# Edge stage of a convolution network: all five maps on VectorE, their sums on ScalarE, weights in batches of one to four images

## The chip, the core and the metric

The kernel runs on one core of one Trainium2 chip, in float32. The metric is the device time of one execution in microseconds. A core has TensorE (PE; its weight loads are shown apart as PEld), VectorE (DVE), ScalarE (ACT), GpSimd (POOL), and SyncE (SP), whose queue issues most DMAs. Each engine runs its own instructions in order and waits for others by semaphores.

## The reference, cut to what matters

The network has a graph layer, a deformable convolution with a state-space scan, a convolution, and last an edge-guided U-shaped network. Only the first layer of that last one, here called the edge stage, is touched. Its input x is 16 images of 32 channels, 128 x 128, after a group norm:

```python
def _norm(x):
    m = jnp.mean(x, axis=(1, 2, 3), keepdims=True)
    s = jnp.std(x, axis=(1, 2, 3), keepdims=True)
    return (x - m) / s

def get_operator(x):
    p3 = ((1, 1), (1, 1))
    p2 = ((1, 0), (1, 0))
    b1 = _norm(0.5 * _corr(x, SOBEL_X, p3) + 0.5 * _corr(x, SOBEL_Y, p3))
    b2 = _norm(0.5 * _corr(x, SCHARR_X, p3) + 0.5 * _corr(x, SCHARR_Y, p3))
    b3 = _norm(_corr(x, LAPLACE3, p3))
    b4 = _norm(0.5 * _corr(x, ROBERTS_X, p2) + 0.5 * _corr(x, ROBERTS_Y, p2))
    b5 = _norm(0.5 * _corr(x, PREWITT_X, p3) + 0.5 * _corr(x, PREWITT_Y, p3))
    return jnp.concatenate([b1, b2, b3, b4, b5], axis=1)
```

These 160 channels go through a 3 x 3 convolution to 32 channels and a 2 x 2 maximum. Every map is a fixed small stencil (with reflected borders), normalised by one mean and one deviation per image and map.

## The kernel before, in words

The network's layers run one after another: `layer0`, `layer1_offsets`, `layer1_scan`, `layer1_sample`, `layer2`, `layer3_edges` (the edge stage), `layer3_net`. Images stand in four groups of four.

The edge stage does not convolve the 160 maps. A stencil followed by a 3 x 3 convolution is one 5 x 5 convolution of x, and normalising a map only scales its part of the weights. So the stage needs, for each image, the mean and variance of the five maps; from these it builds that image's 5 x 5 weights, and convolves x itself with them. Three kinds of work follow:

- Statistics, the generator `stats`. An image is loaded in two strips (h = 0, 1), each a tile `a` with 4 bands of 32 channels on the 128 partitions and 18 rows of 130. From a strip come five maps of 16 x 128 per partition: f1 (Sobel), f2 (Scharr, held in E2), f3 (Laplace), f4 (Roberts), f5 (Prewitt), by way of the sums R, B2, H and differences E1, E2. GpSimd makes E1, E2 and H, VectorE the rest; `keep` runs four bn_stats on each finished map (line 1570), and bn_aggr closes an image. The generator yields after a few operations, so that the caller can place them between convolutions.
- Weights, the function `weights`, for a group of four images: the norm factors (`ms` line 1618, PE averages `pm`, `pv`, a square root on ScalarE), the small diagonal matrices l4 and l5, and twenty matmuls `pw` (lines 1647 and 1648) of the fixed tables base4 and base5, whose results ScalarE copies to Eb and Bb. Then `pr`, `rm`, `pvec`, `pb` give border terms. `expand` copies an image's rows of Eb and Bb by 14 DMAs on SP's queue into W and Wb.
- Convolution of an image: `image` loads it as tile t and scales it on ScalarE (line 1695), `corrections` makes border terms `pc`, `cs`, and `conv` runs eight times: ten matmuls into one of four PSUM buffers `ps` (line 1767), then VectorE adds `cs` at the border columns (line 1785) and takes maxima of pairs into `pl` (line 1786). ScalarE's queue stores `pl` to `p1`.

The driver at the end of `layer3_edges` makes the statistics and weights of group 0, and then, during the convolutions of images 0 to 2 of a group, takes one step of the next group's statistics after an even convolution and two after an odd one; before image 3's convolutions it takes the rest and makes the next group's weights. What the source writes is then placed by a scheduler that lays each engine's instructions in a fixed order of its own, so that operations stand near, but not exactly at, their place in the source. Tile buffers (pool sizes `bufs`) limit how far one engine runs ahead of another.

Of the kernel before, what the change touches and what calls it, by code (L numbers as in the profile page):

```python
# [10 lines left out]
F32 = mybir.dt.float32  # L11
# [6 lines left out]
P = 128  # L18
# [1417 lines left out]
def layer3_edges(tc, w, x3, p1, sb3, b3, groups=range(NG)):  # L1436
# [10 lines left out]
    with ExitStack() as ctx:  # L1447
# [112 lines left out]
        def stats(g, res):  # L1560

            mv = sp.tile([P, 4, 5, 2], F32, name="mv", tag="mv")
            res["mv"] = mv
            nxt = strip(g, 0, 0)
            for j in range(4):
                st = sp.tile([P, 5, 8, 6], F32, name="st", tag="st")

                def keep(i, h, f):
                    for q in range(4):
                        V.bn_stats(st[:, i, 4 * h + q], f[:, 4 * q : 4 * q + 4])  # L1570

                for h in range(2):
                    a = nxt
                    E2 = fp.tile([P, 16, HW], F32, name="E2", tag="e", bufs=2)
                    nc.gpsimd.tensor_sub(E2, a[:, 2:18, 2 : HW + 2], a[:, 0:16, 0:HW])
                    E1 = fp.tile([P, 16, HW], F32, name="E1", tag="e", bufs=2)
                    nc.gpsimd.tensor_sub(E1, a[:, 0:16, 2 : HW + 2], a[:, 2:18, 0:HW])
                    R = fp.tile([P, 18, HW + 1], F32, name="R", tag="R")
                    V.tensor_add(R, a[:, :, 0 : HW + 1], a[:, :, 1 : HW + 2])
                    B2 = fp.tile([P, 17, HW + 1], F32, name="B2", tag="B2")  # L1580
                    V.tensor_add(B2, R[:, 0:17], R[:, 1:18])
                    f1 = fp.tile([P, 16, HW], F32, name="f1", tag="f", bufs=2)
                    V.tensor_sub(f1, B2[:, 1:17, 1 : HW + 1], B2[:, 0:16, 0:HW])
                    yield
                    keep(0, h, f1)
                    f4 = fp.tile([P, 16, HW], F32, name="f4", tag="f", bufs=2)
                    V.tensor_sub(f4, R[:, 1:17, 0:HW], R[:, 0:16, 0:HW])
                    keep(3, h, f4)
                    yield
                    if h == 0:  # L1590
                        nxt = strip(g, j, 1)
                    elif j < 3:
                        nxt = strip(g, j + 1, 0)
                    V.scalar_tensor_tensor(E2, E2, -0.4, f1, ALU.mult, ALU.add)
                    keep(1, h, E2)
                    f5 = fp.tile([P, 16, HW], F32, name="f5", tag="f", bufs=2)
                    V.tensor_sub(f5, B2[:, 0:16, 1 : HW + 1], B2[:, 1:17, 0:HW])
                    V.tensor_add(f5, f5, E1)
                    yield
                    keep(4, h, f5)  # L1600
                    H = fp.tile([P, 18, HW], F32, name="H", tag="H")
                    nc.gpsimd.tensor_add(H, a[:, :, 2 : HW + 2], a[:, :, 0:HW])
                    f3 = fp.tile([P, 16, HW], F32, name="f3", tag="f", bufs=2)
                    V.tensor_add(f3, H[:, 2:18], H[:, 0:16])
                    V.scalar_tensor_tensor(
                        f3, a[:, 1:17, 1 : HW + 1], -4.0, f3, ALU.mult, ALU.add
                    )
                    keep(2, h, f3)
                    yield
                for i in range(5):  # L1610
                    V.bn_aggr(mv[:, j, i], st[:, i])

        def weights(g, mv):


            sc = cb[:, g, :, 0].unsqueeze(2).to_broadcast([P, 4, 5])
            ms = sp.tile([P, 4, 5], F32, name="ms", tag="ms")
            V.tensor_mul(ms, mv[:, :, :, 0], sc)
            vs = sp.tile([P, 4, 5], F32, name="vs", tag="vs")
            V.tensor_mul(vs, mv[:, :, :, 1], sc)  # L1620
            V.tensor_mul(vs, vs, sc)
            pm = psg.tile([P, 4, 5], F32, name="pm", tag="pg")
            nc.tensor.matmul(pm, avg, ms, start=True, stop=True)
            mean = sp.tile([P, 4, 5], F32, name="mean", tag="mean")
# [4 lines left out]
            pv = psg.tile([P, 4, 5], F32, name="pv", tag="pg")  # L1629
            nc.tensor.matmul(pv, avg, ms, start=True, stop=True)  # L1630
            r = sp.tile([P, 4, 5], F32, name="r", tag="r")
# [4 lines left out]
            rs = sp.tile([P, 4, 5], F32, name="rs", tag="rs")  # L1636
            V.tensor_mul(rs, r, isel.unsqueeze(1).to_broadcast([P, 4, 5]))
            r4 = sp.tile([P, 4], F32, name="r4", tag="r4")
            V.reduce_sum(r4, rs, AX.X)
            ey = eye.unsqueeze(1).to_broadcast([P, 4, T])  # L1640
            l4 = sp.tile([P, 4, T], F32, name="l4", tag="l4")
            V.tensor_mul(l4, ey, r4.unsqueeze(2).to_broadcast([P, 4, T]))
            l5 = sp.tile([P, 4, T], F32, name="l5", tag="l5")
            V.tensor_mul(l5, ey, r[:, :, 4].unsqueeze(2).to_broadcast([P, 4, T]))
            for n, ((a, m), (q, o)) in enumerate(zip(cuts, place)):
                pw = psg.tile([P, 480], F32, name="pw", tag="pg")
                nc.tensor.matmul(pw[:, 0:m], l4, base4[:, a : a + m], start=True, stop=False)
                nc.tensor.matmul(
                    pw[:, 0:m], l5[32 * q : 32 * q + 32], base5[32 * q : 32 * q + 32, o : o + m],
                    start=False, stop=True,  # L1650
                )
                if n < 4:
                    nd = m // 160
                    nc.scalar.copy(
                        Eb[:, 3 * n : 3 * n + nd, 3:8],
                        pw[:, 0:m].rearrange("p (d y o) -> p d y o", d=nd, o=T),
                    )
                else:
                    nc.scalar.copy(Bf[:, n - 4], pw[:, 0:m])

            pr = psg.tile([5, P], F32, name="pr", tag="pg")
            for j in range(4):
                nc.tensor.matmul(
                    pr, mean[0:1, j], oneh[:, j], start=(j == 0), stop=(j == 3)
                )
            rm = sp.tile([5, P], F32, name="rm", tag="rm")
            V.tensor_copy(rm, pr)
            pvec = psg.tile([P, 15, T], F32, name="pvec", tag="pg")
            nc.tensor.matmul(pvec, rm, V5, start=True, stop=True)
            vec = sp.tile([P, 15, T], F32, name="vec", tag="vec")  # L1670
            nc.scalar.copy(vec, pvec)
            pb = psg.tile([P, 1], F32, name="pb", tag="pg")
            for j in range(4):
                nc.tensor.matmul(
                    pb[32 * j : 32 * j + 32], V5[:, 14], rm[:, 32 * j : 32 * j + 1],
                    start=True, stop=True, tile_position=(0, 32 * j),
                )
            V.tensor_add(b3[:, g : g + 1], pb, bcol)
# [112 lines left out]
        res = {}  # L1791
        for _ in stats(groups[0], res):
            pass
        vec = weights(groups[0], res["mv"])
        nxt = image(groups[0], 0), *expand(0)
        for m, g in enumerate(groups):
# [3 lines left out]
            for j in range(4):  # L1800
# [3 lines left out]
                elif more:  # L1804
                    for _ in it:
                        pass
# [3 lines left out]
                for n in range(8):  # L1810
# [4 lines left out]
                    if n % 2:  # L1815
                        next(it, None)
# [459 lines left out]
```

## Time and profile before

| | |
|---|---|
| median of 3 runs | 17622.46 us (17619.95 to 17635.37) |
| profiled execution | 17609.38 us, of which the span 17607.6 us |
| PE busy in the span | 15472.8 us (88%) |
| DVE busy | 14994.4 us (85%) |
| ACT busy | 11513.4 us (65%) |
| POOL busy | 10390.4 us (59%) |
| first R of the edge stage (line 1579) | starts at 14888.6 us |
| bn_stats (line 1570) | 640 of them, 395.8 us busy |
| E2, E1, H on POOL (lines 1575, 1577, 1602) | 32 each, means 6662, 5515 and 5790 ns |

All times inside the profile are microseconds from the start of the span, means of one instruction are nanoseconds. A row of a group of instructions reads: line, engine, operation, output and input by name, shapes, count, then busy time and mean of one, then the idle time of the engine just before them and what ended it. A timeline row reads: start, length, engine, line, operation. A row of the stretches reads: stretch, length, then busy time and instruction count of PE, PEld, DVE, ACT and POOL, the granted clock of TensorE as a share of full speed, the busy share of the DMA engines, and GB/s. Matmuls overlap in the pipeline and a float32 matmul shows as two records, so PE's pace is read from starts, not from durations.

### The profile page before, as it was taken

The page shows a single profiled execution, that of the slowest core. Times are in us where ns is not written, and L with a number is a line of the kernel's source. Part 1 is how long each engine was busy: PE and PEld are TensorE (multiplying, and loading weights), DVE is VectorE, ACT ScalarE, POOL GpSimd, SP SyncE. Part 2 cuts the span into 40 slices and gives each one's busy share as a digit, 9 for nine tenths or more (in the row PEclk, how much of TensorE's full clock was granted, in tenths as well). Part 3 has the DMA queues.
Part 4 walks back from the last instruction along what each step waited for, and adds up shares of the span by engine and source line. Part 5 has one row for each costly group of instructions (what it writes and reads, how often), then busy time and mean ns, then how long its engine had stood idle before and what let it go on. Part 6 is the DMA issues. An engine that isn't in the chain of part 4 may idle for free. (4 is left out here: it accounts for less than half of the span.)

```text
span 17607.6 us, 299698 instructions
## 1 busy us (share of the span) xinstructions
PE 15472.8 (88%) x113450; PEld 5973.3 (34%) x113450; DVE 14994.4 (85%) x15134; ACT 11513.4 (65%) x22768; POOL 10390.4 (59%) x18561
## 2 busy tenths in 40 slices
PE   8999999999999888888888888899999976488988
PEld 3333333333333222222222222355555542144433
DVE  9999999999999769999999999788888877999123
ACT  7888888888888556776777777689888952000011
POOL 9999999999999437788888888200000001443000
PEclk9999999999999989999999999889999988699988
DMA  0000000000000664444454445677777788244245
GB/s 21 11 12 11 12 17 11 12 11 12 16 12 7 105 142 157 160 161 156 163 166 164 164 160 167 164 192 199 200 194 195 198 185 173 49 75 73 52 125 174
DMA packets 1519822, 1884.46 MB, mean 107 GB/s; under 512 B 146789, under 2 KB 866717, under 8 KB 1507558
## 3 DMA queue, kind: packets, MB, share of 16 engines
q1 hardware_dynamic: 1413414, 1688.04, 37.2%
q10 hardware_dynamic: 78336, 83.90, 1.5%
q0 software_dynamic: 26624, 93.35, 1.5%
q8 instruction: 892, 14.61, 0.3%
q14 instruction: 556, 4.55, 0.1%
HBM read 1561.58 MB, written 229.64 MB: 102 GB/s over the span
## 5 line engine op out<-in xcount | busy, mean ns | idle before, releaser
L235 POOL TENSOR_SCALAR Rp<-su,nv 128x128 f32<-128x128 f32 x16384 | 5837.5, 374 | 71.7 <-PE pS L241 37.8
L224 DVE TENSOR_TENSOR Rd<-pu,nv 128x2048 f32<-128x2048 f32 x2176 | 4882.9, 2279 | 75.4 <-PE pS L241 71.6
L239 ACT ACTIVATE Ra<-su,bv 128x128 f32<-128x128 f32 x14336 | 4295.0, 395 | 534.6 <-PE pS L241 530.4
L241 PE MATMUL pS<-Rd,zw 128*32 128x512 f32 x17408 | 2910.6, 603 | 214.7 <-DVE Rd L224 214.4
L822 DVE TENSOR_TENSOR_SCAN hh<-dd,state,pd 128x512 f32<-128x512 f32 x2304 | 2823.8, 1267 | 152.0 <-PE py L856 8.5
L843 POOL TENSOR_TENSOR hh<-hh,bc 128x2048 f32<-128x2048 f32 x512 | 2319.9, 4531 | 462.7 <-DVE state L830 452.7
L241 PE MATMUL pS<-Rp,zw 128*32 128x512 f32 x8192 | 2015.9, 597 | 175.6 <-POOL Rp L235 173.6
L1228 POOL DMA_DIRECT2D x<-ob x64 | 90.9, 1420 | 3094.0 <-DVE ob L1227 2757.2
L807 PE MATMUL pd<-du,spread 32*128 32x512 f32 x4608 | 1349.7, 660 | 563.1 <-DVE hh L822 556.0
L799 ACT ACTIVATE dd<-dd,m_a 128x512 f32<-128x512 f32 x2304 | 1518.1, 715 | 358.0 <-DMA dd<-dm 348.6
L817 DVE TENSOR_TENSOR pd<-pd,bc 128x1024 f32<-128x1024 f32 x1152 | 1401.7, 1217 | 55.1 <-ACT bc L780 54.4
L241 PE MATMUL pS<-Ra,zw 128*32 128x512 f32 x7168 | 1278.2, 600 | 0.0
L1236 ACT ACTIVATE yd<-yd,nrow 128x2048 f32<-128x2048 f32 x512 | 1234.5, 2411 | 47.4 <-DMA yd<-ymap 47.4
L1767 PE MATMUL ps<-t,W 128*128 128x512 f32 x2560 | 1170.4, 617 | 88.6 <-DVE pl L1786 88.6
L1116 ACT ACTIVATE ya<-pb,nrow 128x1024 f32<-128x1024 f32 x1024 | 1192.8, 1255 | 74.5 <-PE pb L1115 74.2
L1115 PE MATMUL pb<-Y,sel 32*128 32x512 f32 (+1 forms) x5120 | 1080.9, 741 | 167.5 <-ACT ya L1116 164.3
L241 PEld LDWEIGHTS pS<-Rd,zw 128*32 128x32 f32 x17408 | 624.3, 109 | 1222.1 <-issue 590.6
L807 PEld LDWEIGHTS pd<-du,spread 32*128 32x128 f32 x4608 | 373.4, 191 | 1607.5 <-DVE hh L822 719.0
L1120 DVE TENSOR_SCALAR yd<-yd 128x2048 f32<-128x2048 f32 x512 | 727.0, 1420 | 201.6 <-ACT yd L1236 200.4
L241 PEld LDWEIGHTS pS<-Rp,zw 128*32 128x32 f32 x8192 | 444.6, 110 | 1326.7 <-POOL Rp L235 865.1
L1120 DVE TENSOR_SCALAR ya<-ya 128x2048 f32<-128x2048 f32 x512 | 756.9, 1478 | 10.5 <-ACT ya L1116 9.4
L1767 PEld LDWEIGHTS ps<-t,W 128*128 128x128 f32 x2560 | 498.2, 197 | 724.1 <-issue 723.1
(403 smaller groups left out, 23453.0 us busy)
## 6 DMA issues: line engine op xcount, KB each, us to landing
dd<-dm SPq DMA_DIRECT2D x2304, 256.0 KB
yd<-ymap SPq DMA_DIRECT2D x512, 1024.0 KB
hw<-x SPq DMA_DIRECT2D x192, 512.0 KB
dm<-dt POOLq DMA_DIRECT2D x192, 256.0 KB, 3.6
xb<-tok SPq DMA_DIRECT2D x248, 144.0 KB
w<-d SPq DMA_DIRECT2D x64, 528.1 KB
x<-in_x SPq DMA_DIRECT2D x64, 512.0 KB
x<-o SPq DMA_DIRECT2D x128, 256.0 KB
```

The costliest lines, as they stand in the source:

```text
L224: nc.vector.tensor_tensor(R, st["pu"].unsqueeze(1).to_broadcast([P, 4, 4, HW]), nv[:, :, i::32].rearrange("p t q -> p q t").unsqueeze(3).t ...
L235: nc.gpsimd.tensor_scalar(R[:, q, k], su[:, k], 3.4028234e38, nv[:, k, c], ALU.min, ALU.max)
L239: nc.scalar.activation(R[:, q, k], su[:, k], AF.Relu, bias=bv[:, k, c])
L241: nc.tensor.matmul(st["pS"][32 * q : 32 * q + 32], zw[:, 31 - i : 63 - i], R[:, q], start=first, stop=False, tile_position=(0, 32 * q), sk ...
L799: S.activation(dd[:, r], dd[:, r], AF.Exp, scale=acol[:, dr, d : d + 1])
L807: nc.tensor.matmul(pd[:, a], spread[e, k], st["du"][n][e], start=True, stop=True)
L817: V.tensor_mul(pd, pd, bm.unsqueeze(1).to_broadcast([P, 2, CH]))
L822: V.tensor_tensor_scan(hh[:, r, s], dd[:, r, s], pd[:, a, s], st["state"][:, 4 * i + r : 4 * i + r + 1], ALU.mult, ALU.add,)
L843: G.tensor_mul(hh, hh, st["bc"][1, n].unsqueeze(1).to_broadcast([P, 4, CH]))
L1120: V.tensor_scalar(t, t, 1.0, 1.0, ALU.min, ALU.subtract)
L1236: S.activation(yd, yd, AF.Abs, bias=nrow)
L1767: nc.tensor.matmul(ps, W[:, k, d], t[:, 4 * n + k : 4 * n + k + 4, d : d + HW], start=(i == 0), stop=(i == 9 and n not in (0, 7)), skip_gr ...
```

## The change

In `stats`, the differences f2 and E1 and the sum H move from GpSimd to VectorE, bn_stats and bn_aggr go, and ScalarE makes for each map its sum (an Identity with an accumulated output), the negative mean of the strip's map, and the sum of squared deviations (a Square with that bias, accumulated). Six small VectorE operations per image combine the two strips into mean and variance. Maps have five buffers in place of two and two. The next strip is loaded a strip ahead.

`weights` takes a range of images instead of a group, with outputs at those images' partitions only. The driver runs over single images; the batches are image 0, 1, 2-3, 4-5, 6-7, 8-11 and 12-15. A batch is made after the fifth convolution of the image before it, after the statistics it needs; two steps of the statistics follow each convolution, up to a pace that is set for images from 6 on.

```diff
-                    nc.gpsimd.tensor_sub(E2, a[:, 2:18, 2 : HW + 2], a[:, 0:16, 0:HW])
-                    nc.gpsimd.tensor_sub(E1, a[:, 0:16, 2 : HW + 2], a[:, 2:18, 0:HW])
...
-                        V.bn_stats(st[:, i, 4 * h + q], f[:, 4 * q : 4 * q + 4])
...
-                    nc.gpsimd.tensor_add(H, a[:, :, 2 : HW + 2], a[:, :, 0:HW])
...
-                    V.bn_aggr(mv[:, j, i], st[:, i])
+                def keep(i, f):
+                    nm = sp.tile([P, 1], F32, name="nm", tag="nm", bufs=4)
+                    nc.scalar.activation(f, f, AF.Identity, accum_out=sq[:, 0, h, i : i + 1])
+                    nc.scalar.mul(nm, sq[:, 0, h, i : i + 1], -1.0 / (16 * HW))
+                    nc.scalar.activation(
+                        f, f, AF.Square, bias=nm, accum_out=sq[:, 1, h, i : i + 1]
+                    )
+                R = made("R", 18, HW + 1)
+                V.tensor_add(R, a[:, :, 0 : HW + 1], a[:, :, 1 : HW + 2])
+                f4 = made("f")
+                V.tensor_sub(f4, R[:, 1:17, 0:HW], R[:, 0:16, 0:HW])
+                keep(3, f4)
+                yield
+                B2 = made("B2", 17, HW + 1)
+                V.tensor_add(B2, R[:, 0:17], R[:, 1:18])
+                f1 = made("f")
+                V.tensor_sub(f1, B2[:, 1:17, 1 : HW + 1], B2[:, 0:16, 0:HW])
+                yield
+                f2 = made("f")
+                V.tensor_sub(f2, a[:, 2:18, 2 : HW + 2], a[:, 0:16, 0:HW])
+                V.scalar_tensor_tensor(f2, f2, -0.4, f1, ALU.mult, ALU.add)
+                keep(0, f1)
+                keep(1, f2)
+                yield
+                E1 = made("f")
+                V.tensor_sub(E1, a[:, 0:16, 2 : HW + 2], a[:, 2:18, 0:HW])
+                f5 = made("f")
+                V.tensor_sub(f5, B2[:, 0:16, 1 : HW + 1], B2[:, 1:17, 0:HW])
+                yield
+                V.tensor_add(f5, f5, E1)
+                keep(4, f5)
+                H = made("R", 18, HW + 1)[:, :, 0:HW]
+                V.tensor_add(H, a[:, :, 2 : HW + 2], a[:, :, 0:HW])
+                yield
+                f3 = made("f")
+                V.tensor_add(f3, H[:, 2:18], H[:, 0:16])
+                V.scalar_tensor_tensor(
+                    f3, a[:, 1:17, 1 : HW + 1], -4.0, f3, ALU.mult, ALU.add
+                )
+                keep(2, f3)
+                yield
...
-        def weights(g, mv):
+        def weights(b0, b1, mv):
+            g, j0 = divmod(b0, 4)
+            n = b1 - b0
+            e = slice(32 * j0, 32 * (j0 + n))
...
+                nc.tensor.matmul(
+                    pw[e, 0:m], l4, base4[:, a : a + m], start=True, stop=False,
+                    tile_position=(0, 32 * j0),
+                )
...
+        images = [4 * g + j for g in groups for j in range(4)]
+        mv = cp.tile([P, 4, 2, 5], F32, name="mv", tag="mv")
+        it = stats(images, mv)
+        made = 0
+        cut_at = [0, 1, 2, 4, 6, *range(8, len(images), 4), len(images)]
...
+        def batch(m):
+            end = min(c for c in cut_at if c > m)
+            advance(12 * end + 1)
+            return weights(images[m], images[end - 1] + 1, mv)
+        vec = batch(0)
+        nxt = image(*divmod(images[0], 4)), *expand(0)
+        for m, b in enumerate(images):
...
+                t1 = image(g1, j1)
+                if m + 1 not in cut_at:
+                    nxt = t1, *expand(j1)
+            cs = corrections(j, t, W, Wb, v)
+            for n in range(8):
...
+                conv(n, j, t, W, Wb, v, cs, pl)
+                if m < 6 or made < 12 * (m + 2) + 3 * n:
+                    advance(min(made + 2, 12 * len(images) + 1))
+                if n == 4 and m + 1 < len(images) and m + 1 in cut_at:
+                    vec = batch(m + 1)
+                    nxt = t1, *expand(j1)
```

## The prediction

> **What bounds the kernel now.** The change touches one stage, the edge stage, so I first looked for where it lies: the chain of work that ended last, in order of time. Columns are start, length, what.
>
> ```profile
> 14880.16 7.65 DMA a<-x
> ...
> 15206.82 3.92 DVE ms L1618
> 15259.31 9.94 PE ps L1767 x20
> ...
> 16501.53 60.43 PE ps L1767 x140
> ...
> 16659.49 60.43 PE ps L1767 x140
> ```
>
> The stage starts with a strip load at 14880, its first convolution matmul is at 15259, its last ends at 16659.5 + 60.4 = 16719.9. The busy time of the engines in stretches of the stage shows who is the limit (length, then PE, PEld, DVE, ACT, POOL busy with instruction counts, granted clock, DMA share, GB/s):
>
> ```profile
> 14860.00:15206.00 346.00, 0.00 (x0) 0.00 (x0) 333.32 (x330) 11.85 (x24) 174.71 (x31) 0.50 0.28 45
> 15206.00:15256.00 50.00, 35.09 (x53) 12.12 (x54) 31.32 (x38) 5.36 (x13) 20.40 (x4) 0.50 0.22 42
> ...
> 15794.00:15940.00 146.00, 116.99 (x388) 55.91 (x387) 145.99 (x128) 5.49 (x9) 67.19 (x25) 0.90 0.42 73
> 15940.00:16173.00 233.00, 226.42 (x650) 103.12 (x650) 201.28 (x204) 20.90 (x35) 77.85 (x32) 0.95 0.43 80
> ...
> 16320.00:16723.00 403.00, 400.99 (x1190) 185.63 (x1190) 48.26 (x115) 23.65 (x28) 6.58 (x43) 0.97 0.23 47
> ```
>
> For 346 us VectorE alone makes the statistics of the first four images and PE does nothing. Each later group costs about 380 us (first stall at 15405, the next at 15794, then 16173), because VectorE must finish the next group's statistics; only the last five images run at PE's own pace. That pace is the distance of the x140 rows: (16659.49 - 16423.24) / 3 = 78.7 us an image. ScalarE is nearly idle. The groups of instructions of this stage, with shapes:
>
> ```profile
> L1570 DVE BATCH_NORM_STATS2 st<-f 128x6 f32<-128x512 f32 x512 | 316.5, 679 | 0.0
> ...
> L1579 DVE TENSOR_TENSOR R<-a 128x2322 f32<-128x2322 f32 x32 | 131.5, 4109 | 26.6 <-ACT a L1557 26.6
> ```
>
> And the VectorE timeline, where one strip (half an image) can be priced from start to start:
>
> ```profile
> 15099.55 2.28 DVE L1587 TENSOR_TENSOR f<-R 128x2048 f32<-128x2048 f32 x1
> 15101.75 4.84 DVE L1570 BATCH_NORM_STATS2 st<-f 128x6 f32<-128x512 f32 x8
> ```
>
> One 2048-element operation occupies VectorE 2.20 us, one bn_stats 4.75 / 8 = 0.6 us. A strip now takes 38.57 us (the R at 15007.87 to that at 15085.01 is two strips, 77.14).
>
> **The change part by part.**
>
> *VectorE.* Removed per strip: 20 bn_stats, 12 us, and the waits and slow rows beside GpSimd (R takes 2.55 us alone, 4.11 on average). Added: f2, E1 and H on VectorE. A strip becomes twelve operations: R 2.55, B2 2.35 (both read from the stretch at 15204), H about 2.5 (2304 elements, between them), nine at 2.20: 27.2 us, 11.4 less. Six tiny operations per image replace five aggregations, about 1 us each way: nothing.
>
> *ScalarE.* Five maps per strip, each an Identity and a Square with an accumulated sum, and a tiny scaling. No accumulating activation is in this trace. The nearest row is the 128x2048 Identity of the last stage (L2015, 2.09 us), the tiny row 0.2 us (the square root, L1632, 0.19). Lower bound: 2 x 2.09 + 0.2 = 4.4 us a map, 22 us a strip; upper bound, a tiny instruction more for each sum, and a bubble: 5.0 us, 25 us a strip. I take 22 to 23. With strip edges (0.45) and the image scaling (3.94 + 0.5 per two strips) it stays at or under VectorE's 27.2, so it hides beside it; at 25 it would add about 1 us a strip in the fill only, since both are under PE's 39 us per strip later. At the end of a batch its last map adds 4 to 5 us.
>
> *GpSimd* loses all three maps, and with them nothing that anyone waits for.
>
> *Fill.* Only image 0 is needed before its weights. Count from the first R (14888.6). Two strips end at 54.4. The built program puts the norms of image 0 into the third strip, behind seven of its maps: first norm operation (ms) at 71.5, and l4, with stats operations of 2.2 to 2.5 us between its steps, at 92. From l4 to the first convolution the trace has 15259.1 - 15221.3 = 38 us: twenty weight matmuls, one after another, in 31.9, then rm, pvec, pb, corrections. So the first convolution is at 130 (before: 370.5). The fill gives 240 us.
>
> *Between batches.* This is where I expect much of it to go back. Before, the weights of a group were made while image 3 of the last group still had five convolutions to run. In the built program PE's order is fixed: the first norm matmul pm of the batch of images 2-3 stands behind all of image 1's convolutions, and that of images 8-11 behind all of image 7's; for images 4-5 and 6-7 the second one (pv) stands behind the last convolution; for images 12-15 pm stands 0.6 of a convolution before the end, and only image 1's weights lie among convolutions. So PE waits for its own weights:
> - image 1: pw in line (16 us warm, as in the groups later in the trace) and 7 for rm, pvec, pb: 23.
> - images 2-3: ms at 316 (strip 7 is held behind convolution 1.3, at 276, and the norms come in strip 8), 16 for hops to l4, 38: convolution at 370, 55 after image 1's end.
> - images 4-5: square root and 3 us of hops, 38: 43. Images 6-7, one stats operation more: 45.
> - images 8-11: 24 of the units of the statistics, four strips, are asked for at once in image 7; strips 22 and 23 (54.4) and nine convolution evictions in order put ms at 962, 18 after image 7's end, then 16 + 38: 73.
> - images 12-15: VectorE has no strips left and PE is warm: 16 for pw and 6 for rm, pvec, pb: 22.
>
> Sum 261. Each restart runs cold for about 8 us (the clock of 0.50, then 0.93, after 15256), 4 us lost, five times: 20.
>
> [...] In the window 15206 to 15256 the weight matmuls ran at a granted clock of 0.50 throughout, 1.97 us for two passes of 480 columns:
>
> ```profile
> 15223.57 1.96 PE L1648 MATMUL pw<-base,l 32*128 32x480 f32 x2
> 15225.47 1.97 PE L1647 MATMUL pw<-base,l 128*128 128x480 f32 x2
> ```
>
> [...] The row says 31.9. [...] I take the row[...].
>
> *Sum.* First convolution 130; sixteen images at 78.7, 1259; gaps 261; restarts 20: 1670, that is 16559, against 16720: 161 us less. The profiled execution took 17609.4 (span 17607.6), so 17448; the median of the runs shown, 17622.5, is 13 above it: 17461, I say 17460. If the cover of the convolutions were complete, 261 would shrink to 6 batches x 16 us of matmuls, a gain of about 330.
>
> *DMA queues and ScalarE's order.* The strips come one earlier in SP's queue; each waits for the strip two before, which VectorE has finished by then, so no weight copy (14 DMAs per image, as before, 7.4 us for the W ones) stands behind a blocked load for long. The p1 stores on ScalarE's queue now wait for VectorE in front of the map sums; the maps have five buffers, and VectorE is itself waiting for PE there: nothing. bound: 0 to 4 us an image if not.
>
> **The rivals.**
> 1. *The chains are shorter* (weights warm, or stats operations hide the hops): 14 us less in four chains, 10 less in two: 17385; with complete cover 17290. For: the pw rows later in the trace take 1.07 us. Against: PE idles before each.
> 2. *ScalarE's queue becomes the chain* (slower): every batch needs twelve ScalarE steps (square root, ten weight copies, vec), and now a map's pair of activations (4.4 us) can stand before each. 7 x 12 steps, a whole pair each: 370 us, that is 17460 + 370 - some 150 which the cold matmuls cover: 17680. It decides from 161 / 84 = 1.9 us of wait per step. Against it: in the built order the ten copies stand together in four of the seven batches, and two PSUM buffers let PE run one ahead.
> 3. *The change does nothing*: the statistics move from VectorE to ScalarE, and the accumulated sums cost so much (over 7.8 us a map, 39 us a strip) that ScalarE holds PE back as VectorE did. Then about 17620. Nothing in the ScalarE rows comes near that.
>
> **How the numbers follow.** The main case 0.62, rival 1 0.26, rival 2 0.07, rival 3 0.05. The main case's own range is 17400 to 17540 (upper map cost and 10 us more per chain above, half of the chains warm below). Reaching into rival 1, the range is 17340 to 17560. What a measurement of this kernel can tell from no change is about 0.2%, 35 us. Rivals 2 and 3 give slower 0.07 and same 0.05; faster 0.88.
>
> **What would show it.** Right: first convolution near 15019; strips of 27 us on VectorE; bn_stats gone; PE idle for 40 to 75 us before images 2, 4, 6 and 8, with a clock of 0.50 in the weight matmuls; image pace 78.7. Wrong: a map's pair over 5 us on ScalarE, PE waiting for Eb or Bb copies that stand behind map sums, VectorE waiting for map buffers, or images slower than 79 us outside the gaps. A time under 17340 would mean that the weights are made under convolutions; over 17590, that ScalarE's queue is in the chain.

## The result, and the profile after

The changed kernel took 17406.5 us (median of four runs, 17404.0 to 17410.2) against 17621.2 us for the kernel before on the same chip: a ratio of 0.988, with a 95% interval of 0.986 to 0.989. That is 215 us less. The profiled execution took 17404.0 us (span 17402.1).

Almost all of it lies where the change is. I call "the stage" the stretch from the start of the first R to the start of the last convolution matmul. The lines of the two operations (count, then duration in ns as minimum, median and maximum, then first and last start) in the trace before:

```profile
L1579 DVE TENSOR_TENSOR R<-a x32: 2508/3420/6193, 14888.6 to 16294.4; 128x2322 f32<-128x2322 f32 x32
L1767 PE MATMUL ps<-t,W x2560: 590/592/1223, 15259.1 to 16719.3; 128*128 128x512 f32 x197
```

So the stage took 1830.7 us. In the trace after:

```profile
L1586 DVE TENSOR_TENSOR R<-a x32: 2540/2570/2580, 14887.3 to 16141.1; 128x2322 f32<-128x2322 f32 x32
L1794 PE MATMUL ps<-t,W x2560: 590/592/1222, 15010.7 to 16516.1; 128*128 128x512 f32 x197
```

It is now 16516.1 - 14887.3 = 1628.8 us, 201.9 less. The spans differ by 205.5. The other 9 of the 215 come from which execution was profiled: before, it lay 12 us under its median, now 2.5.

The stretches of the stage after (length; PE, PEld, DVE, ACT and POOL busy with counts; granted clock, DMA share, GB/s):

```profile
14860.00:14978.00 118.00, 1.18 (x4) 1.00 (x4) 105.31 (x129) 72.72 (x93) 0.80 (x4) 0.50 0.53 82
14978.00:15010.00 32.00, 30.96 (x49) 4.67 (x49) 21.03 (x14) 15.55 (x26) 0.00 (x0) 0.50 0.26 55
...
15200.00:15242.00 42.00, 34.12 (x59) 8.36 (x59) 19.23 (x19) 18.25 (x28) 0.00 (x0) 0.50 0.15 32
15242.00:15395.00 153.00, 153.00 (x466) 71.93 (x466) 132.02 (x101) 101.59 (x129) 2.04 (x10) 0.97 0.47 84
...
15793.00:15872.00 79.00, 38.71 (x69) 14.30 (x70) 65.67 (x52) 53.98 (x71) 0.57 (x3) 0.52 0.50 90
...
16207.00:16520.00 313.00, 311.24 (x974) 146.49 (x973) 28.22 (x66) 13.88 (x13) 5.50 (x39) 0.98 0.26 52
```

The 346 us at the head of the stage in which PE did nothing have become 118. Then PE alternates: convolutions of two images with PE busy all the time at a clock of 0.97 (15242 to 15395), and between them holes of 35 to 79 us in which it makes its own weights at about half clock (15200 to 15242: 34 of 42 us busy, at 0.50). The longest hole, ahead of images 8 to 11, has only 38.7 of 79 us busy. In the last line PE has nothing but convolutions.

The groups of instructions show who now does the statistics:

```profile
L1581 ACT ACTIVATE f<-f,nm 128x2048 f32<-128x2048 f32 x160 | 319.4, 1996 | 7.5 <-DMA p<-pl 3.9 <-ACT nm L1580 1.0
L1579 ACT ACTIVATE f<-f 128x2048 f32<-128x2048 f32 x160 | 304.6, 1904 | 300.3 <-DVE f L1588 138.9 <-DVE f L1598 110.5 <-DVE f L1607 25.9
L1586 DVE TENSOR_TENSOR R<-a 128x2322 f32<-128x2322 f32 x32 | 82.3, 2571 | 13.5 <-DMA a<-x 12.2 <-ACT a L1557 1.1
...
L1579 ACT ACTIVATION_READ_ACCUMULATOR f<-f 128x1 f32 x160 | 29.9, 187 | 0.0
```

R takes 2571 ns, 4109 before, and its spread is gone (2540 to 2580 ns above). With the maps back on GpSimd, in an experiment below, R spreads from 2502 to 6405 ns again. ScalarE needs about 4.1 us a map (in its timeline a round of Identity, Square, their two reads and the tiny scaling starts at 14914.89 and is over at 14918.98), and the last column of the L1579 row says that it waits 300 us for VectorE's maps: it has slack.

One chain between batches, that of images 2 and 3, in PE's timeline:

```profile
15192.67 0.60 PE L1647 MATMUL pm<-ms,avg 128*128 128x10 f32 x2 [6.43 <-DVE ms L1643]
15199.92 0.60 PE L1653 MATMUL pv<-ms,avg 128*128 128x10 f32 x2 [6.65 <-DVE ms L1651]
15208.02 1.86 PE L1668 MATMUL pw<-base,l 128*64 128x480 f32 x2 [7.49 <-DVE l L1663]
15209.81 1.86 PE L1672 MATMUL pw<-base,l 32*64 32x480 f32 x2
...
15241.87 3.76 PE L1794 MATMUL ps<-t,W 128*128 128x512 f32 x4
```

Three hops of about 7 us to VectorE and back, in which PE is idle, then 30 us of weight matmuls and 4 us of the border terms behind them. The bracket names the wait before a row.

### The profile page after: what moved, and what is told of

Same layout as the page of the kernel before. It is cut to its first block, busy times and chain, and to the rows that moved or that the text cites. A ratio compares the mean times of both kernels' runs of the same rounds, so it can differ in the third digit from the quotient of the medians.

```text
span 17402.1 us, 300113 instructions
## 1 busy us (share of the span) xinstructions
PE 15532.7 (89%) x113588; PEld 5966.0 (34%) x113588; DVE 14616.2 (84%) x14651; ACT 12173.3 (70%) x23604; POOL 9783.9 (56%) x18465
## 5 line engine op out<-in xcount | busy, mean ns | idle before, releaser
L1127 PE MATMUL pd<-ya,xt 128*32 128x128 f32 x16384 | 690.7, 311 | 41.9 <-DVE ds L1280 30.0
```

## The experiments

A part of every time is not the edge stage's doing: what lies ahead of the first R is the same in all these kernels, and took between 14845 and 14963 us in the profiled executions. One kernel alone, run twice (e11 and e13), showed 14939 and 14853, with mean granted clocks of 0.941 and 0.944; what made the difference was not settled. So I put the stage beside the times. It is taken from one execution of each kernel, but it repeats well: 1628.8 and 1632.1 for the changed kernel, 1535.3 and 1537.2 for the other one that ran twice. Each ratio is to the kernel before on the same chip, whose median there was 17602 to 17621 us. The labels are explained where the experiments are told.

| kernel | time, us (lowest to highest) | ratio to before (interval) | stage, us |
|---|---|---|---|
| before | 17621.2 | 1 | 1830.7 |
| changed | 17406.5 (17404.0 to 17410.2) | 0.9877 (0.986 to 0.9894) | 1628.8 |
| e1_groups | 17428.0 (17410.2 to 17433.8) | 0.9894 (0.9879 to 0.9909) | 1656.4 |
| e2_old_maps | 17615.0 (17581.4 to 17663.8) | 1.0007 (0.9994 to 1.002) | 1837.9 |
| e3_half_weights | 17340.9 (17323.2 to 17386.8) | 0.985 (0.9833 to 0.9868) | 1558.9 |
| e4_busy | 17419.0 (17399.0 to 17427.4) | 0.9889 (0.9874 to 0.9904) | 1650.3 |
| e5_pace | 17368.2 (17349.6 to 17403.7) | 0.9851 (0.9816 to 0.9886) | 1617.1 |
| e6_early1 | 17395.1 (17381.8 to 17409.8) | 0.9864 (0.983 to 0.9898) | 1628.1 |
| e8_more_act | 17450.6 (17419.0 to 17510.9) | 0.9901 (0.9865 to 0.9938) | 1684.5 |
| e9_full_rows | 17349.7 (17307.3 to 17356.7) | 0.9833 (0.9798 to 0.9868) | 1568.4 |
| e10_full_early1 | 17351.6 (17336.3 to 17418.9) | 0.9855 (0.9836 to 0.9874) | 1567.7 |
| e11_full_pace | 17358.2 (17323.3 to 17365.9) | 0.9856 (0.9836 to 0.9877) | 1535.3 |
| e12_changed_again | 17409.7 (17393.1 to 17420.5) | 0.9884 (0.9867 to 0.9902) | 1632.1 |
| e13_both_again | 17295.0 (17281.1 to 17320.7) | 0.9823 (0.9807 to 0.9839) | 1537.2 |

### The two halves of the change

The change does two things: other engines for the statistics, and smaller batches. Each was taken alone.

```diff
-        cut_at = [0, 1, 2, 4, 6, *range(8, len(images), 4), len(images)]
+        cut_at = [*range(0, len(images), 4), len(images)]
```

> The changed kernel with one part undone: batches are whole groups of four images (0-3, 4-7, 8-11, 12-15) again; maps on VectorE and sums on ScalarE stay. Theory A (the fill is shortened by the split, and most of the split's gain is given back in the weight chains that PE waits for): the first convolution comes after eight strips instead of two and a half, 220 + 17 + 38 = 275 us after the first R instead of 123, so 152 later; but of the six chains between batches, 250 us with their restarts in the changed kernel, three remain, of about 56, 25 and 25. Time about 17406 + 152 - 140 = 17420, within 30. Theory B (the chains between batches cost little, the split is the gain): about 150 slower than the changed kernel, 17555.

Measured 17428.0, a stage of 1656.4. The move of engines with batches of four gives 1830.7 - 1656.4 = 174 of the 202. The first convolution came 288 us after the first R instead of 123, yet the stage ended only 28 later: the small batches save 165 in the fill and pay 137 of it back, in three more chains with PE idle or at half clock. That is theory A (17420 forecast, 17428.0 measured).

The other half: the driver and batches of the change, but the maps of before (E1, E2, H on GpSimd, bn_stats and bn_aggr on VectorE).

```diff
-                    nc.scalar.activation(f, f, AF.Identity, accum_out=sq[:, 0, h, i : i + 1])
...
+                        V.bn_stats(st[:, i, 4 * h + q], f[:, 4 * q : 4 * q + 4])
...
+                nc.gpsimd.tensor_sub(E2, a[:, 2:18, 2 : HW + 2], a[:, 0:16, 0:HW])
```

> The changed kernel with the other part undone: maps E1, E2, H on GpSimd and bn_stats on VectorE as before, in the new driver with its batches of one to four images. A strip costs VectorE 38.6 us again, 77 an image, and with the evictions 84 against PE's 78.7. Theory A: VectorE is the bound from the first batch to the last one; first convolution about 140 us after the first R, the last batch's norms after 32 x 38.6 + 12 x 5.6 + some 120 of waits at rm = 1420, the end at 1420 + 25 + 315 = 1760 instead of 1629: 130 slower than the changed kernel, 17535. Theory B (only the split matters, the engine move is hidden): within 20 of 17406.

Measured 17615.0: no difference from before. This missed my 17535, and the trace says why:

```profile
L1582 DVE TENSOR_TENSOR R<-a x32: 2502/3056/6405, 14887.4 to 16328.0; 128x2322 f32<-128x2322 f32 x32
```

```profile
15500.00:15800.00 300.00, 248.62 (x677) 101.87 (x678) 266.04 (x270) 22.46 (x45) 98.05 (x34) 0.78 0.38 68
```

The first convolution starts at 134 (before 370.5), but the last strip starts 1440.6 us after the first, against 1405.8 before: VectorE, busy for 266 of 300 us, sets the end, and PE that starts earlier only waits more often, at a clock of 0.78. In the changed kernel the last strip starts at 1253.8. Here a head start was worth something only once the engine that feeds PE had become faster: alone, the engines give 174 us and the batches lose 7, together they give 202.

Which part of the engines' move counts was not tried separately. An estimate from the rows of the two traces: a strip loses 12.4 us of bn_stats (395.8 / 32), and 6.6 us by which R, B2 and the maps were longer beside GpSimd, and gains about 7 for three more maps.

### Is ScalarE near being the bound?

One more pass over every map:

```diff
+                    nc.scalar.activation(f, f, AF.Identity)
                     nc.scalar.activation(
                         f, f, AF.Square, bias=nm, accum_out=sq[:, 1, h, i : i + 1]
```

> Edit: one more pass of ScalarE over every map (an identity of 128x2048, some 1.9 us, ahead of the squares), which adds 9.5 us a strip to the 22 that ScalarE has now; nothing else is changed. Theory A (ScalarE has slack: VectorE's 27 us a strip set the pace of the fill, TensorE the pace after it): strips become 32 us of ScalarE, so the fill grows by about 5 us a strip for two strips and a chain waits some us more at its end: 20 to 40 more than the changed kernel, 17425 to 17445. Rival B (ScalarE is in the chain of the steps, since VectorE waits for map buffers that it gives back): 9.5 us a strip over the 32 strips less what is hidden, more than 100: over 17510.

Measured 17450.6; the stage is 56 longer, between the two forecasts and nearer to slack: 160 passes of 1.9 us are 303 us more work, of which over four fifths are hidden. What is not hidden shows the mechanism of my second rival at work. In the chain of images 4 and 5, pv is done at 15420, but its square root on ScalarE comes only at 15429.0, behind two maps' worth of passes; the reciprocal on VectorE then waits its turn until 15441.4, and PE stands still. ScalarE's timeline, then VectorE's, then PE's:

```profile
15428.92 0.19 ACT L1582 ACTIVATION_READ_ACCUMULATOR f<-f,nm 128x1 f32 x1
15429.01 0.16 ACT L1655 ACTIVATE r<-pv 128x10 f32<-128x10 f32 x1
```

```profile
15441.36 0.21 DVE L1656 RECIPROCAL r<-r 128x10 f32<-128x10 f32 x1
```

```profile
15446.47 1.86 PE L1669 MATMUL pw<-base,l 128*64 128x480 f32 x2 [21.95 <-DVE l L1664]
```

In the changed kernel the same wait before pw was 2.26 us. So the rival's path exists, but the changed kernel stays short of it.

### Why do the weight matmuls run at half clock?

In the changed kernel, five of the seven weight chains ran at a granted clock of 0.50 through 28 to 32 us of uninterrupted matmuls (that of images 4 and 5 after its first two). First, the second matmul of each pair (the one on l5 and base5, with 32 rows) left out, which leaves one of the five maps out of the weights:

```diff
-                nc.tensor.matmul(
-                    pw[e, 0:m], l5[32 * q : 32 * q + 32], base5[32 * q : 32 * q + 32, o : o + m],
-                    start=False, stop=True, tile_position=(32 * q, 32 * j0),
-                )
```

> The changed kernel without the second matmul of each weight cut (the fifth map's part of the weights is left out), so ten weight matmuls per batch instead of twenty. Theory A (the weight matmuls stand on the path at half clock in five chains): 15 us less in each of five chains, 7 in the two that run warm: 90 less, 17316. Theory B (the chain is paced by ScalarE's copies, which stand behind the map sums): 20 less at most.

Measured 17340.9, 70 off the stage: nearer to theory A's 90 than to B's 20. Half as many matmuls at half clock would be about 15 us a chain; the first chain took 9, and the clock rose in it:

```profile
14965.00:14970.00 5.00, 3.47 (x5) 0.85 (x6) 5.00 (x4) 3.86 (x7) 0.00 (x0) 0.50 0.28 39
14970.00:14975.00 5.00, 4.90 (x15) 1.12 (x14) 5.00 (x3) 3.31 (x8) 0.00 (x0) 0.99 0.29 58
```

With matmuls of 128 rows alone the clock of this chain was 0.50 in the first stretch and 0.99 in the next; in the changed kernel, where every second matmul has 32 rows, it stayed at 0.50 through the whole chain (28.6 us, 14978.5 to 15007.1).

Second, matmuls with no use for their result, behind pm (four) and behind pv (five), to keep PE at work through the hops:

```diff
+            busy(4, vs)
...
+            busy(5, ms)
```

> The changed kernel with nine more matmuls of 480 columns per batch into an unused PSUM bank, four after pm and five after pv, where PE otherwise waits for VectorE's norms. Theory A (the weight matmuls run at a clock of 0.50 because PE idled just before them; kept busy, it is warm): the weight matmuls of the batches for images 2, 4, 6 and 8 fall from 31 to 16-20 us, some 50 us less in all, 17355, less what the extra ones delay (0 to 15). Theory B (these matmuls never raise the clock, whatever stands before): the clock stays at 0.50 in them, and the time is 17406 to 17425.

Measured 17419.0, the stage 21 longer. The time lies where theory B had it, but the clock is neither theory's. Two chains ran at full clock. Images 4 and 5, straight behind a convolution:

```profile
15403.93 1.02 PE L1678 MATMUL pw<-base,l 128*64 128x480 f32 x2
15404.88 1.01 PE L1682 MATMUL pw<-base,l 32*64 32x480 f32 x2
```

That chain took 16.1 us instead of 28, and that of images 6 and 7, straight behind the added matmuls, 15.9 instead of 30. But images 2 and 3, where the added matmuls ended at 15202 and PE then waited 3.3 us (clock 1.00 from 15202 to 15206):

```profile
15205.31 1.02 PE L1678 MATMUL pw<-base,l 128*64 128x480 f32 x2 [3.30 <-DVE l L1673]
15206.26 1.86 PE L1682 MATMUL pw<-base,l 32*64 32x480 f32 x2
```

One matmul at full speed (1.02 us), then 0.50 to the end of the chain (15206 to 15234). So in this run the two chains that came without a break kept a full clock, and the one behind 3.3 us lost it. How soon is not settled: behind the same pause of 2.26 us the chain of images 4 and 5 lost it within 2 us in the changed kernel, but only after 9 us, and a second pause of 1.4, in e5 below (the 480-column matmuls of the two-image batches had a mean of 887 ns there, 985 in the changed kernel). And what these two chains won was less than what the added matmuls cost in other places: counted from the first R, image 8 started 8 us later than in the changed kernel and image 12 about 22.

Third, the rows alone. The left side becomes a block whose other 96 rows are zero, the right side takes all rows of the same columns; four small multiplies take the place of one:

```diff
-                    pw[e, 0:m], l5[32 * q : 32 * q + 32], base5[32 * q : 32 * q + 32, o : o + m],
-                    start=False, stop=True, tile_position=(32 * q, 32 * j0),
+                    pw[e, 0:m], l5m[:, q, 0:n], base5[:, o : o + m],
+                    start=False, stop=True, tile_position=(0, 32 * j0),
```

> Edit: the second matmul of each pair in the weight chain (pw) reads all 128 rows instead of 32: its left side is a block whose other 96 rows are zero, its right side the whole of the same columns. Four small VectorE multiplies take the place of one, everything else as in the changed kernel. Theory A (the clock is not raised because every second matmul uses a quarter of the rows; with the half-weights kernel, where only full-row matmuls were left, it rose after about 5 us): the twenty matmuls now raise the clock, a chain takes about 16 to 18 us instead of 31 in the first, second, third, fourth and fifth batch, about 14 us less each, so 60 to 70 less than the changed kernel: 17340. Rival B (the half-weights chain was shorter because it had half the matmuls and the clock rose for another reason, such as fewer weight loads): the clock stays at 0.50, chains of 31 us, 17405 plus some 2 for the added multiplies.

Measured 17349.7, 60.4 off the stage. The first chain, still twenty matmuls:

```profile
14986.05 1.81 PE L1673 MATMUL pw<-base,l 128*32 128x480 f32 x2 [5.48 <-DVE l L1666]
14987.65 1.81 PE L1677 MATMUL pw<-base,l5m 128*32 128x480 f32 x2
...
14990.85 1.50 PE L1677 MATMUL pw<-base,l5m 128*32 128x480 f32 x2
14992.18 0.97 PE L1673 MATMUL pw<-base,l 128*32 128x480 f32 x2
14992.99 0.97 PE L1677 MATMUL pw<-base,l5m 128*32 128x480 f32 x2
```

From 1.81 to 0.97 us within about 6 us of its start, and the chain is through in 16. The number of matmuls and of loads, and the columns, are those of the changed kernel; what differs in the chain is the rows that the second of each pair and its load span. The pause ahead of the chain is shorter too (5.5 us, 9.2 in the changed kernel), but that does not tell the two apart: 13 chains of 32-row pairs that began at half clock and ran unbroken (one in the kernel before, four in the changed kernel, three in e6, five in e8) kept that speed to their end behind pauses of 2.4 to 22 us, with 1.7 to 1.9 us from one 480-column matmul to the next (0.93 at full clock). So in these traces the clock rose in chains of full rows, and not in chains with 32 rows in every second matmul. Whether their number makes the difference, or where the 32 lie (`tile_position`), was not tried separately.

Not all of the gain is the clock. At full clock in both kernels, two such matmuls start 0.81 us apart here (14992.18 to 14992.99), and 0.93 in the changed kernel's chain among the convolutions of image 0 (15082.62 to 15083.55). Over twenty matmuls that is 2 to 3 us of the 9 to 15 that a chain lost.

### What the holes hold besides

The pace that holds the statistics back for images from 6 on, removed:

```diff
-                if m < 6 or made < 12 * (m + 2) + 3 * n:
+                if True:
```

> Edit: in the changed kernel the condition that lets the strips' maps be issued between the convolutions is made always true, so the steps of a batch are issued one by one from its first convolution on and never gathered in a burst. Theory A (the 25 us in which TensorE idles ahead of the batch of images 8 to 11 are VectorE's late steps): the idle time ahead of that batch's first mean matmul falls from 25 us to below 10, and 15 less in all: 17390. Rival B (VectorE has no free time to catch up; what is taken from this gap is lost at the other ones, since the same strips come later): within 5 of 17405.

The stage is 11.7 shorter, as theory A had it. The time fell by 38, but 42 us of difference in this profiled execution lie ahead of the first R, so only the stage is evidence. What it removed is PE's wait ahead of images 8 to 11, in the last column of the group of pm with 20 columns (the two batches of four images), here of the changed kernel and of this one:

```profile
L1647 PE MATMUL pm<-ms,avg 128*128 128x20 f32 x4 | 1.0, 334 | 25.1 <-DVE ms L1643 25.1
```

```profile
L1647 PE MATMUL pm<-ms,avg 128*128 128x20 f32 x4 | 0.9, 307 | 8.2 <-DVE ms L1643 8.2
```

Of these 17 us, 6 are lost again ahead of images 12 to 15: image 12 starts 102.4 us after image 11, in the changed kernel 96.2.

With the steady pace, a batch asked for earlier:

```diff
-                if n == 4 and m + 1 < len(images) and m + 1 in cut_at:
+                if n == (4 if m < 2 else 1) and m + 1 < len(images) and m + 1 in cut_at:
```

> Edit: as the steady pace, and from the third image on the chain of the next batch is issued after the second convolution of the last image of a batch instead of after the fifth. Theory A (a chain costs its full length because TensorE reaches it with nothing left to do while it waits; convolutions of the same image placed behind the start of the chain cover its waits and keep the clock up): of each of five gaps (35 to 79 us) the waits of about 15 to 20 and part of the 15 us of half clock go, 60 to 90 less: 17330. Rival B (TensorE takes its work in order, so that matmuls of the chain that wait hold up the convolutions behind them, and VectorE's steps for the batch, asked for earlier, are late): 17400 to 17440.

A stage of 1628.1, 11 longer than with the pace alone. The early chains did pay at first: image 6 started 722.4 us after the first R, with the pace alone 745.1. But the norms of images 8 to 11 came no sooner: their pm stands at 918.7 us, with the pace alone at 914.4. In between PE now waits for VectorE to empty the PSUM buffers of image 7:

```profile
15773.11 11.08 PE L1794 MATMUL ps<-t,W 128*128 128x512 f32 x20 [9.37 <-DVE pl L1813]
15796.27 11.45 PE L1794 MATMUL ps<-t,W 128*128 128x512 f32 x20 [12.08 <-DVE pl L1813]
```

So VectorE sets the start of that batch, as rival B had it. The time, 17395.1, lies just under B's range; the 60 to 90 of theory A did not come.

### A better version

> Edit: full rows in the weight chain and the steady pace together. From the first map addition to the last convolution the edge stage took 1629 us in the changed kernel, 1568 with full rows (60 less) and 1617 with the steady pace (12 less). Theory A (the two are separate: one shortens the matmuls of a chain, the other VectorE's lateness ahead of the batch of images 8 to 11): 72 less, a stage of 1557 and a time of about 17335. Rival B (a shorter chain of the batches before makes VectorE later still at images 8 to 11, so the pace only takes back what full rows lost there): 1565 to 1570, and 17345.

The stage was 1535.3, 93 less than the changed kernel: more than the 72 of theory A, against which B had less. So the two are not separate: with full rows the pace is worth 33 us, without them 12. The waits of pm show why. With full rows alone they are 36 us, against 25 in the changed kernel, and the two batches of four stand one by one below: the shorter chains made VectorE late at images 8 to 11 (28.4 us) and now at images 12 to 15 too (7.8); this part of rival B was right:

```profile
L1650 PE MATMUL pm<-ms,avg 128*128 128x20 f32 x4 | 1.2, 391 | 36.2 <-DVE ms L1646 36.2
```

```profile
15772.72 0.62 PE L1650 MATMUL pm<-ms,avg 128*128 128x20 f32 x2 [28.38 <-DVE ms L1646]
...
16132.40 0.61 PE L1650 MATMUL pm<-ms,avg 128*128 128x20 f32 x2 [7.79 <-DVE ms L1646]
```

Behind the second wait the whole chain of images 12 to 15 lay open, begun at half clock (the pm above took 0.61 us, 0.40 in the changed kernel), where the changed kernel had it at a clock of 1.00 among the last convolutions: image 12 came 103.5 us after image 11 instead of 96.2. With the pace as well, 10 us of wait are left (from the repeat of this kernel further on), none of it at image 12, which came 95.4 us after image 11:

```profile
L1650 PE MATMUL pm<-ms,avg 128*128 128x20 f32 x4 | 0.9, 308 | 10.2 <-DVE ms L1646 10.2
```

The time of 17358.2 did not show the 93; in the profiled execution the stage began at 14939, 52 later than in that of the changed kernel.

> Edit: full rows in the weight chain, the steady pace, and from the third image on the chain of the next batch issued after the second convolution of the last image of a batch instead of after the fifth. With the changed kernel's matmuls this early chain gave nothing (stage 1628 against 1629, where the pace alone gave 1617), since chains issued early wait for VectorE with convolutions behind them. Theory A (VectorE's steps set the start of a chain, so that asking earlier only moves the wait): stage of 1565 to 1575, no better than full rows with the pace alone, 17345. Rival B (with shorter chains the convolutions behind them cover the hops between VectorE and TensorE): stage of 1530, 17305.

A stage of 1567.7, 32 longer than with full rows and the pace: theory A. An early chain did not pay even when it was short; PE waits 9.4 and 12.0 us for VectorE in image 7, as before.

To see whether the gain is real in the time, the changed kernel and the version with both edits ran side by side on one chip:

> The changed kernel itself, unaltered, beside the next kernel on one chip, so that the two can be set against each other: the part ahead of the edge stage, which is the same in all of these kernels, took from 14845 to 14963 us in the profiled executions so far and blurs the times. Both theories: a stage of 1629 us (first map addition to the start of the last convolution's matmul), and a time of 17406.

> Full rows in the weight chain and the steady pace together, unaltered from the run before, beside the changed kernel. Theory A (the stage of 1535 us against 1629 is the true difference and the smaller one of the times comes from what lies ahead of the stage): a stage of 1535 again, and a time 60 to 95 below that of the changed kernel on the same chip. Rival B (a faster edge stage costs something elsewhere, so that the time gains only about 48 as the medians of different chips had it): 40 to 50 below, with a stage again of 1535 and the part ahead of it again some 50 later.

Stages of 1632.1 and 1537.2, as before, and times of 17409.7 and 17295.0: 115 apart, with ranges that are far from touching. Theory A had at most 95. In the profiled executions, which are 132 apart, 95 are the stage, and 41 lie ahead of it in favour of the second. I do not count these as its doing: in e11, the same kernel, that part took 14939 us, more than the 14894 of the changed kernel here. What the two edits are shown to give is the 95 of the stage. This version beats both kernels: 0.9823 of the kernel before (0.9807 to 0.9839), where the changed kernel beside it had 0.9884 (0.9867 to 0.9902). As e11, on another chip, it had 0.9856.

## Why the prediction was right, and where its terms were off

The prediction said 17460 and faster; it was 17406.5. Its main case is what happened, and the sum missed the stage by 41 us, the change of the profiled execution by 44 and the median by 54. The last 10 are the step "the median is 13 above the profiled execution", which after the change was 2.5. In the profiled execution the gain was thus about a quarter larger than forecast. The miss of 41 comes from four terms of the sum: 7 us in the fill, 22 in the chains and restarts, 6 in the pace of an image, and 6 in the last image, which was counted at a full pace though nothing follows it.

- **VectorE, 27.2 us a strip.** R starts at 14887.27, 14914.78 and 14942.35: 27.5. Right.
- **ScalarE, 4.4 us a map.** 4.1: the Identity took 1904 ns and the Square 1996 where I had 2090 from the row L2015, and each accumulated sum is indeed a further instruction (187 ns, half of it overlapped). Hidden, as said; the doubled pass showed how far.
- **First convolution at 130.** It came at 123.4. The norms were where the built program put them (ms at 71.6, 71.5 predicted) and pw began at 91.2 (92). Mis-sized was the step from l4 to the convolution, "38 us" taken from the group of four before: 32.2.
- **The chains, 23, 55, 43, 45, 73, 22.** By the distance of two images' starts, less a pace of 78.3: image 1 20, images 2-3 54, 4-5 31, 6-7 36, 8-11 75, 12-15 18. The first of these holds its restart; the other restarts cost about 6 us each, not 4. The places and the causes were right. At images 8-11 the 18 us of lateness were 25. Most of the 22 us lie at images 4-5 and 6-7: the step of "38" was 32 and 34 there (37 at images 8-11, a group of four like the one it was taken from), and more of the hops was hidden behind the last convolutions. At image 1 I counted the border terms beside an image's pace that holds them already.
- **Pace 78.7.** The last images took (16456.26 - 16299.69) / 2 = 78.3.
- **End at 1670.** The last matmul ended at 16516.7, 1629.4 after the first R.

**The row.** I took the pace of the weight matmuls from the trace before (twenty in 31.9 us, at a clock of 0.50), and for this kernel that was right: the chains stayed at 0.50 for 28 to 32 us. That it carries over to the new batches was an estimate that no trace had shown, and there the prediction was lucky: it held for pairs with 32 rows in the second matmul. With full rows and the same columns the matmuls ran at full speed from 3 to 6 us after the start of 11 chains that began at half clock (two of e9, four of e11, five of e13). That full rows then took 60 off the stage, where the first rival's 14 us in four chains make 56, is in part chance: the chains of five batches, not four, became 9 to 15 us shorter, some of it without the clock, and 10 us of the 70 won by image 8 were lost again by the end.

**The rivals.** Shorter chains (17385) was half true: the matmuls ran at 0.50 again, but the hops at images 4-5 and 6-7 were more hidden and the tail was shorter, and the largest piece of the miss lies there. ScalarE in the chain (17680) did not happen, and its path became visible only with 9.5 us more per strip. That nothing changes needed 7.8 us a map, and it was 4.1; but "nothing" is what the split alone gives.

## What to carry to other kernels

Starting the consumer earlier, in smaller batches, paid here only once the producer was faster: the batches alone gave 0 and the faster producer alone 174 of 202 us. Even then a chain that the engine must wait for is paid at each batch, and most of the head start went back. Before shortening such a chain, look at the granted clock in it: here every second matmul used a quarter of the rows, the whole chain ran at 0.50, and filling the rows with zeros won 60 us. PE, asked earlier for what VectorE had not finished, only waited elsewhere, as the early chains showed (9.4 and 12.1 us in image 7). And where the stages ahead vary by 100 us between executions, compare the stage, not the total.

## What the runs showed of the hardware that I had not expected

- In chains of alternating matmuls of 128 and 32 rows the granted clock did not rise in this stage: the 13 chains counted above, which began at half clock and ran unbroken, kept that speed for their 28 to 32 us (clock 0.50 in every such chain of the two kernels). Where all matmuls had 128 rows, they ran at full speed from 3 to 6 us after the start, in 11 chains (e9, e11, e13), and in e3 the clock was 0.50 in one stretch of 5 us and 0.99 in the next. Alternating matmuls that began at full clock without a pause kept it for 16.9 us (three chains of the kernel before, and that of images 12 to 15 in the changed kernel, where the clock was 1.00); behind pauses of 2.26 us (changed kernel) and 3.30 us (e4) it was lost within 2 us, behind 2.26 us in e5 after 9. This is what these chains showed, not what every mix does: elsewhere in the changed kernel's trace the clock went from 0.50 (11215.9 to 11219.3) to 1.00 (11219.3 to 11222.7) with 32-row matmuls (pb) among 128-row ones (pd).
- At full clock, a matmul of 480 columns started 0.93 us after its neighbour where every second one had 32 rows (changed kernel, 15082.62), and 0.81 where all had 128 (e9, 14992.18).
- Each accumulated sum on ScalarE is an instruction of its own in the changed kernel's trace, 187 ns, and hardly counts, since about half of it overlaps with the next one (14905.31 and 14905.40).
- VectorE's 128x2048 operation on float32 took 2.20 us with GpSimd idle (before, 15099.55 to 15101.75); the R of the same strips went from 4.11 to 2.57 us when GpSimd's maps were taken away, and spread from 2.5 to 6.4 us when they came back (e2). In the trace before, an R that started at 15311.77, while GpSimd made E1 until 15313.72, ended 2.4 us after E1; GpSimd's H, started at 15313.68, ended 3.9 us after that R, where a map of nearly this size had taken 3.8 with VectorE idle (15306.13).
